# A four-layer graph network on one core: one more block by product in the last layer, and a rearranged preparation

## The chip, the core and the metric

The kernel runs on one core of a Trainium2 chip. The core has a matrix engine (TensorE, called PE in the profile, with its weight loads shown apart as PEld), three engines that work on elements (VectorE: DVE, ScalarE: ACT, GpSimd: POOL) and a queue that only issues transfers (SyncE: SP). The metric is the device time of one execution in microseconds; lower is better. The kernel before takes 2123.33 us (median of three runs, 2122.25 to 2134.76).

## The reference

There are 6250 nodes with 256 channels and 100,000 edges, sorted by destination. The input is normalised and passed through a relu; then come four graph layers, and the result is added to the input:

```python
def agg(h):
    return jax.ops.segment_sum(h[src], dst, num_segments=N)
for l in range(NL - 1):
    h = x + agg(x)
    h = jax.nn.relu(h @ W1s[l] + b1s[l])
    h = jax.nn.relu(h @ W2s[l] + b2s[l])
    x = h @ W3s[l] + b3s[l]
h = x + agg(x)
h = jax.nn.relu(h @ cW1 + cb1)
h = jax.nn.relu(h @ cW2 + cb2)
return h @ cW3 + cb3
```

All of it is float32. `NL` is 4, so three equal layers and a last one with a middle of 64 channels.

## The kernel before

**Blocks.** The nodes lie in 49 blocks of 128. The first product with W1 is pulled ahead of the sum over edges, so what a layer adds up over the edges is already a node's row times W1 (`w31` is the product of one layer's W3 and the next one's W1, made in the preparation by `fused`). A layer's rows stay on the chip in `XY`, each as a high part and a remainder, and also go to a table in memory, `tables[l]`.

**Two ways to sum over the edges.** For most blocks of destinations the kernel builds a matrix of edge counts (a destination block against all 49 source blocks, one byte an element) and multiplies it with `XY`. The matrices are built once, beside layer 0, by one-hot products (`build`: one-hots `lo` and `hi` at L1053 on DVE, products `bp` at L1094 on PE, casts to bytes at L1102 on ACT and L1104 on DVE), are used there where layer 0 needs them, and are stored in `mats` for the later layers (L1109). A layer reads them back in chunks (`fetch`, L1127), casts them (`prepare`, L1598) and multiplies: by panels of four blocks (`product`, L1700, 196 products of 128x512 for a panel), or for a single block (`product_by_node`, L1622, 49 products). In layer 0 all products are by node.

For the other blocks the rows of the sources are gathered from the table: 17 indirect transfers of 128 rows for each block, issued by POOL (`send`, L1407), and added up by PE with small one-hot products (`add`, L1446: 46 instructions, called a visit). `gone` lists the blocks whose edges are prepared for that, `solos[l]` those of them that layer l multiplies as single blocks instead. Gathered are 23 blocks in layer 0, 20 in layers 1 and 2, and 19 in layer 3 (blocks 0 to 17 and 48), where 18 and 19 are single products.

**Order of the work.** The order of instructions on each engine is written out when the program is made. One unit of time is one cast of a matrix piece and the products that use it; `tick` runs what is due in it: visits, turns (L1506), the layers' further products (`mlp`: L1248 or L1256, then L1268 or L1313) and stores. A clock in the model, `clock`, counts the costs of what PE has been given (`passed`). By it the gathers of a layer are asked for evenly: `begin` takes the model's work of the layer (`work_of`), less `TAIL[l]` and a margin of 6, less what has passed since the layer's first product, and divides it by the number of gathers. Each gather waits for the PE instruction at its place (`after`). A visit is due 6 us of model time after its last gather is asked for, at the latest `LATE[l]` units from the end of the layer's units. When all rows of a layer are in its table, the next layer's gathers begin.

For layer 3 the model's work before the change is 444.3 us: 30 blocks x 49 products of 512 columns, 19 visits and turns of 3.4, 45 + 5 blocks of further layers (19.35 + 8.6) and 7.8 for starts. With TAIL 10 it has 323 gathers to place. For layers 1 and 2, with 29 blocks, 20 visits and TAIL -5, it is 496.0 and 492.6, with 340 gathers.

**The preparation.** `look` finds the edges of each block by comparisons and asks for them; its last step turns the positions and indices (PE at L848) into `rel` and `idx` (DVE at L855 and L858), which the gathers need. Beside it `normed` goes through the blocks in pairs, one pair a step: moments (L892, L893), square root (L898), scale (L904, L905, L912), transposes (L921), product with W1 (L933), copy to `zs` (L945), high part (L949, ACT), remainder (L953, DVE), store to the table (`keep`, by SP). After the last pair's product, ten products whose result is not used stand in PE's queue (L939). The buffers of the preparation are given back when its last store has landed; the first one-hot of the gathers (L1430) and the building use that memory. The first 24 casts of the building all run on ACT.

`spare` is the memory of the positions `clT`, reused later for a few single results and the last layer's weights. Tiles named `align` only shift addresses.

## Time and profile before

| | us |
|---|---|
| median of three runs | 2123.33 |
| lowest and highest of them | 2122.25, 2134.76 |
| the profiled execution | 2128.08 |
| its span, first to last instruction | 2126.3 |
| PE busy, mean granted clock | 2034.3, 0.99 |

The profile shows one execution. Its times are microseconds from the first instruction. A group of instructions has a line of the code, an engine, an operation, its output and input, the shape and the count, then the busy time, the mean length of one in nanoseconds, and the idle time of the engine just before it, with what ended most of that. A row in order of time has start, length, engine, line and operation; what stands in brackets is the idle time before it and what ended it. The table by stretches gives, for each engine, its busy time in the stretch and its number of instructions, then the clock that was granted to PE (1.00 is full), the share of time in which the transfer engines were busy, and what they moved.

### The profile page before, as it was taken

How to read it: one execution, taken by the hardware profiler on the slowest of the kernel's cores; microseconds unless marked ns; L12 is line 12 of the kernel's file. 1: busy time of each engine (PE TensorE's matmuls, PEld its weight loads, DVE VectorE, ACT ScalarE, POOL GpSimd, SP SyncE). 2: the span in 40 equal slices, each digit the busy share in tenths (PEclk: the TensorE clock that was granted, in tenths of full speed). 3: DMA queues.
4: the chain of work that ended last, by engine and by line, in shares of the span. 5: the costliest groups of instructions: out<-in, count | busy, mean ns of one | idle time of the engine just before them, and what ended most of it. 6: DMA issues, size and time to landing. Idle time of an engine off the chain costs nothing.

```text
span 2126.3 us, 33236 instructions
## 1 busy us (share of the span) xinstructions
PE 2034.3 (96%) x12076; PEld 1495.9 (70%) x12076; DVE 925.0 (44%) x2103; ACT 872.8 (41%) x1793; POOL 1445.9 (68%) x1467
## 2 busy tenths in 40 slices
PE   6889999999999999999999999999999999989998
PEld 4657676667676777777777777777776767766665
DVE  6987767677662422232234322322233323223333
ACT  5766656456555433323233423232233322222222
POOL 3747777677774477777777477777776477777772
PEclk9989999999999999999999999999999999999999
DMA  5534455545455654555566554555555555555563
GB/s 174 159 117 148 145 156 150 157 139 162 140 161 168 205 163 145 160 177 161 154 184 202 171 165 149 176 166 158 169 171 176 173 170 185 161 184 185 154 189 109
DMA packets 184900, 347.54 MB, mean 163 GB/s; under 512 B 32446, under 2 KB 118496, under 8 KB 184726
## 3 DMA queue, kind: packets, MB, share of 16 engines
q0 software_dynamic: 68960, 185.36, 29.9%
q1 hardware_dynamic: 113838, 158.12, 22.8%
q8 instruction: 96, 1.57, 0.3%
q10 hardware_dynamic: 1928, 1.85, 0.3%
q14 instruction: 78, 0.64, 0.1%
HBM read 287.93 MB, written 57.26 MB: 162 GB/s over the span
## 4 chain that ended last, share of the span: by engine, by line
PE 86%; DMA 4%; DVE 3%; issue 1%; ACT 1%; POOL 1%; DVEq 0%; SPq 0%; POOLq 0%; ACTq 0%
PE agg L1700 43%; PE agg L1622 15%; PE sums L1446 11%; PE ps L1256 6%; PE ps L1313 6%; PE bp L1094 4%; DMA rows<-table,idx 4%; PE ps L1506 1%; DVE hi L1053 1%; POOL rows L1407 1%; DVE at L1104 1%; PE ps L1268 1%; PE ps L1248 0%; DVE lo L1053 0%; ACT at L1102 0%
## 5 line engine op out<-in xcount | busy, mean ns | idle before, releaser
L1407 POOL DMA_INDIRECT rows<-table,idx x1394 | 1388.8, 996 | 595.7 <-issue 225.7
L1700 PE MATMUL agg<-a,XY 128*128 128x512 f32 x4116 | 978.6, 395 | 1.9 <-DVE clT L1634 1.9
L1700 PEld LDWEIGHTS agg<-a,XY 128*128 128x128 f32 x4116 | 764.9, 188 | 192.7 <-issue 35.0
L1598 ACT CAST a<-at 128x512 fp32r<-128x512 uint8 (+1 forms) x542 | 328.7, 617 | 653.7 <-PE agg L1700 613.1
L1598 DVE CAST a<-at 128x512 fp32r<-128x512 uint8 x543 | 246.8, 456 | 515.7 <-PE agg L1700 479.1
L1622 PE MATMUL agg<-XY,a 128*128 128x512 f32 x1470 | 405.4, 410 | 1.7 <-ACT a L1582 1.0
L1622 PEld LDWEIGHTS agg<-XY,a 128*128 128x128 f32 x1470 | 260.0, 190 | 51.4 <-issue 6.6
L1446 PE MATMUL sums<-rows,hot 128*32 128x256 f32 x3772 | 248.3, 391 | 33.5 <-DMA rows<-table,idx 33.3
L1446 PEld LDWEIGHTS sums<-rows,hot 128*32 128x32 f32 x3772 | 124.0, 111 | 151.0 <-DMA rows<-table,idx 46.1
L1582 ACT CAST a<-at 128x512 fp32r<-128x512 uint8 (+2 forms) x362 | 197.2, 576 | 6.6 <-PE agg L1622 6.6
L1102 ACT CAST at<-bp 128x392 uint8<-128x392 f32 x252 | 121.5, 490 | 186.9 <-PE bp L1094 181.3
L1104 DVE CAST at<-bp 128x392 uint8<-128x392 f32 x228 | 128.6, 564 | 137.4 <-PE bp L1094 135.0
L1475 DVE TENSOR_TENSOR u<-u,sums 128x256 f32<-128x256 f32 x82 | 34.4, 419 | 301.3 <-PE agg L1700 273.6
L1094 PE MATMUL bp<-hi,lo 128*128 128x196 bf16 x960 | 128.3, 256 | 14.9 <-DVE hi L1053 13.3
L1313 PE MATMUL ps<-w,h 128*128 128x256 f32 x588 | 133.8, 379 | 1.4 <-ACT h L1259 0.9
L1053 DVE TENSOR_TENSOR hi<-cols,pairs 128x784 bf16<-128x784 bf16 x240 | 134.9, 562 | 0.0
L1256 PE MATMUL ps<-h,w 128*128 128x512 f32 (+3 forms) x332 | 133.8, 545 | 0.3 <-ACT h L1713 0.3
L1094 PEld LDWEIGHTS <-lo 128*128 128x128 bf16 x960 | 72.3, 100 | 83.5 <-DVE hi L1053 34.9
L1313 PEld LDWEIGHTS ps<-w,h 128*128 128x128 f32 x588 | 111.3, 190 | 18.5 <-ACT h L1259 1.4
L1321 DVE TENSOR_TENSOR zz<-ps,w 128x512 f32<-128x512 f32 (+1 forms) x75 | 50.2, 679 | 116.5 <-PE ps L1313 116.5
L1053 DVE TENSOR_TENSOR lo<-lanes,pairs 128x512 bf16<-128x512 bf16 x240 | 100.6, 419 | 0.7 <-issue 0.3
L1510 ACT ACTIVATE h<-ps,bias 128x256 f32<-128x256 f32 (+1 forms) x116 | 47.6, 464 | 128.5 <-PE ps L1506 128.5
(170 smaller groups left out, 962.6 us busy)
## 6 DMA issues: line engine op xcount, KB each, us to landing
at<-mat SPq DMA_DIRECT2D x151, 448.0 KB
mat<-at SPq DMA_DIRECT2D x30, 784.0 KB
rows<-table,idx POOLq DMA_INDIRECT x1394
table<-zz SPq DMA_DIRECT2D x72, 256.0 KB
back<-table SPq DMA_DIRECT2D x99, 128.0 KB
xs<-in_x_dram SPq DMA_DIRECT2D x8, 768.0 KB
table<-zs SPq DMA_DIRECT2D x24, 256.0 KB
out_dram<-zz SPq DMA_DIRECT2D x24, 256.0 KB
```

Of the source, the lines that this page charges most:

```text
L1053: nc.vector.tensor_tensor(o.rearrange("p q (n t) -> p q n t", t=2), values.rearrange("p (n t) -> p n t", t=2)[:, None, :, :].to_broadcast( ...
L1094: mm = nc.tensor.matmul(bp[:, m * HW:(m + 1) * HW], lo[:, q + m, :], hi[:, q + m, :], start=True, stop=True)
L1102: nc.scalar.copy(o, v)
L1104: nc.vector.tensor_copy(o, v)
L1256: mm = nc.tensor.matmul(ps[:mp, :w], weights[l][0][:, c, i * P:i * P + mp], h1[:, c, :w], start=(c == 0), stop=(c == KC - 1))
L1313: mm = nc.tensor.matmul(o, h2[0][:, c, nodes], w3[:, c, :], start=(c == 0), stop=(c == KC - 1))
L1407: got = nc.gpsimd.indirect_dma_start(out=t, out_offset=None, in_=tables[self.l][:, :], in_offset=bass.IndirectOffsetOnAxis(ap=idx[:, o:o + ...
L1446: nc.tensor.matmul(self.sums[m * Q:(m + 1) * Q, :C], self.hot[:, c - min(rounds), m, :], self.rows[g, c + 4 * m], start=(c == ROUNDS[0][0] ...
L1582: nc.scalar.copy(a[:, i * m * P:(i + 1) * m * P].rearrange("p (j d) -> p j d", j=m), counts[b][:, j:j + m, :])
L1598: cast(o, at[:, :, d:d + m * P])
L1622: mm = nc.tensor.matmul(agg, a[:, d:d + P], XY[:, j, :], start=(j == 0), stop=(j == NT - 1))
L1700: mm = nc.tensor.matmul(agg[c][:, :w], XY[:, j, o:o + P], a[:, :w], start=(at == 0 and half == 0), stop=(at == NT - 1 and half == 1))
```

## The change

**In the last layer** block 17 becomes a single product as well: `solos[3]` is 17, 18, 19, and 18 blocks are gathered, with 306 transfers. Its product stands behind that of the first panel. In the model the layer's work is then 452.4 us (31 blocks of products, 18 visits). `TAIL` of layer 3 goes from 10 to -3 and its `LATE` from -8 to -5; `TAIL` of layer 0 goes from 10 to 16.

**Beside layer 0** block 17's matrix is built too, as the 26th of 31, and the four blocks that are built only for later layers come at other places in the order.

**In the preparation** the moments of six blocks are put together in four operations of their own where each block had an aggregation; the high part, the remainder and the store are done for four blocks at a time; of the weights for the fused products one has a single buffer and is loaded after its last use; and the ten unused products behind the last pair become sixteen behind the turning of positions and indices.

```diff
-    solos = [[], [19], [19], [18, 19]]
+    solos = [[], [19], [19], [17, 18, 19]]
...
     for i in range(panels[-1][1]):
-        made.insert(6 * i + 5, panels[-1][0] + i)
+        made.insert((4, 9, 14, 19)[i], panels[-1][0] + i)
+    made.insert(25, 17)
...
     def fused(pool, w3_aps, w1_aps):
-        loaded = []
-        def load(l):
-            if l < NLAYER:
-                loaded.append((load_w("w3", w3_aps[l], pool, nc.scalar, bufs=2),
-                               load_w("w1n", w1_aps[l], pool, nc.scalar, bufs=2)))
-        load(0)
+        def left_of(l):
+            return load_w("w3", w3_aps[l], pool, nc.scalar, bufs=1) if l < NLAYER else None
+        def right_of(l):
+            return load_w("w1n", w1_aps[l], pool, nc.scalar, bufs=2) if l < NLAYER else None
+        w3, w1 = left_of(0), right_of(0)
         yield
         for l in range(NLAYER):
-            w3, w1 = loaded[l]
-            load(l + 1)
+            w1_next = right_of(l + 1)
...
                 nc.scalar.copy(w3t[:, k, :], ps[:, :C])
+            w3 = left_of(l + 1)
             yield
...
                 nc.vector.tensor_copy(o, ps[:, :left[NQ]])
+        still = ps_m.tile([P, W], F32, name="ps")
+        for _ in range(16):
+            nc.tensor.matmul(still, XY[:, 1, :P], XY[:, 0, :], start=True, stop=True)
         yield
...
         def moments(s):
             i0, n = pairs[s]
+            t0 = i0 // G * G
+            if i0 == t0:
+                each[t0] = pool.tile([P, G, 6], F32, name="stats", bufs=2)
             for i in range(i0, i0 + n):
-                stats = pool.tile([P, nc.vector.BN_STATS_DIM], F32, name="stats", bufs=4)
-                nc.vector.bn_stats(stats, xs[i // G * G][:, i % G, :])
-                nc.vector.bn_aggr(mv[:, i, :], stats)
+                nc.vector.bn_stats(each[t0][:, i - t0, :], xs[t0][:, i - t0, :])
             if (i0 + n) % G == 0 or i0 + n == NT:
...
+                nc.vector.tensor_tensor(apart[:, :m], v[:, :m, 1], v[:, :m, 4], OP.subtract)
+                nc.vector.tensor_tensor(both[:, :m, :], v[:, :m, 1:3], v[:, :m, 4:6], OP.add)
+                nc.vector.scalar_tensor_tensor(apart[:, :m], apart[:, :m], float(C // 4),
+                                               apart[:, :m], op0=OP.mult, op1=OP.mult)
+                nc.vector.tensor_tensor(both[:, :m, 1], both[:, :m, 1], apart[:, :m], OP.add)
                 std = pool.tile([P, G], F32, name="std", bufs=2)
-                nc.scalar.activation(std[:, :m], mv[:, t0:t0 + m, 1], AF.Sqrt, bias=eps)
+                nc.scalar.activation(std[:, :m], both[:, :m, 1], AF.Sqrt, bias=eps, scale=1.0 / C)
...
             paced[:] = [mm.ins.name]
-            if s == len(pairs) - 1:
-                still = ps_m.tile([P, W], F32, name="ps")
-                for _ in range(10):
-                    nc.tensor.matmul(still, XY[:, 1, :P], XY[:, 0, :], start=True, stop=True)
...
         def out(s):
-            zs[s] = pool.tile([P, 2, C], F32, name="zs", bufs=4)
+            i0, n = pairs[s]
+            if s % 2 == 0:
+                zs[s] = pool.tile([P, 4, C], F32, name="zs", bufs=3)
+            o = zs[s - s % 2][:, s % 2 * 2:s % 2 * 2 + n, :]
...
+        def four(s):
+            if s % 2 == 0 and s + 1 < len(pairs):
+                return None
+            i0 = pairs[s - s % 2][0]
+            return i0, pairs[s][0] + pairs[s][1] - i0, s - s % 2
+
         def high(s):
-            i0, n = pairs[s]
-            nc.scalar.copy(XY[:, i0:i0 + n, :C], zs[s][:, :n, :])
+            if four(s):
+                i0, n, k = four(s)
+                nc.scalar.copy(XY[:, i0:i0 + n, :C], zs[k][:, :n, :])
...
-        order = [[]] + [[0, 1, 2, 19, 3, 4, 5, 6]] * 2 + [[0, 1, 18, 2, 3, 19, 4, 5, 6]]
+        order = [[]] + [[0, 1, 2, 19, 3, 4, 5, 6]] * 2 + [[0, 17, 1, 18, 2, 3, 19, 4, 5, 6]]
...
-        TAIL = [10.0] + [-5.0] * (NLAYER - 1) + [10.0]
-        LATE = [-8] + [10] * (NLAYER - 1) + [-8]
+        TAIL = [16.0] + [-5.0] * (NLAYER - 1) + [-3.0]
+        LATE = [-8] + [10] * (NLAYER - 1) + [-5]
...
                 u = alone[l, b0] = late.tile([P, C], F32, name="us", bufs=1) if (
-                    k == 1) else spare[:, k // 2 * C:(k // 2 + 1) * C]
+                    k == 1) else spare[:, 3 * (k // 2) * C:(3 * (k // 2) + 1) * C]
...
-            rings.tile([P, 64], U8, name="align", bufs=1)
+            rings.tile([P, 192], U8, name="align", bufs=1)
...
-        rings.tile([P, 128], U8, name="align", bufs=1)
```

31 lines of the change are left out of this document (18 added, 13 removed).

## The prediction, made before the change was run

> **What bounds the kernel now.** The head of the page and its chain of waits come first.
>
> ```profile
> span 2126.3 us, 33236 instructions
> ...
> PE 2034.3 (96%) x12076; PEld 1495.9 (70%) x12076; DVE 925.0 (44%) x2103; ACT 872.8 (41%) x1793; POOL 1445.9 (68%) x1467
> ...
> PE 86%; DMA 4%; DVE 3%; issue 1%; ACT 1%; POOL 1%; DVEq 0%; SPq 0%; POOLq 0%; ACTq 0%
> ```
>
> TensorE (PE) is busy for 96% of the span and carries 86% of the chain, so an added product costs its length, and a gain has to come from stages where PE waits. The table by stretches shows where: the gathering parts of layers 1, 2 and 3 (columns: start:end, length, busy time of PE, its weight loads, DVE, ACT and POOL, granted clock, DMA share, GB/s).
>
> ```profile
> 735.00:1175.00 440.00, 439.59 (x2541) 328.38 (x2540) 132.64 (x278) 140.03 (x252) 321.79 (x327) 1.00 0.55 168
> 1215.00:1642.00 427.00, 422.05 (x2457) 313.19 (x2456) 124.71 (x263) 133.31 (x240) 321.64 (x325) 1.00 0.55 168
> 1690.00:2098.00 408.00, 381.66 (x2323) 279.24 (x2322) 124.02 (x253) 113.59 (x202) 303.41 (x306) 0.98 0.56 173
> ```
>
> In layer 1 PE idles 0.4 us of 440, in the last layer 26.3 of 408. The groups of PE in these three stretches name the waiter, the gathered sums (count, busy time, mean ns, idle before); the fourth row, also of the last stretch, is the product of the two single blocks.
>
> ```profile
> L1446 PE MATMUL sums<-rows,hot 128*32 128x256 f32 x920 | 56.6, 381 | 0.1
> ...
> L1446 PE MATMUL sums<-rows,hot 128*32 128x256 f32 x920 | 58.6, 382 | 4.9 <-DMA rows<-table,idx 4.9
> ...
> L1446 PE MATMUL sums<-rows,hot 128*32 128x256 f32 x874 | 66.6, 414 | 26.0 <-DMA rows<-table,idx 26.0
> L1622 PE MATMUL agg<-XY,a 128*128 128x512 f32 x98 | 23.5, 393 | 0.0
> ```
>
> An undisturbed visit of a block takes 56.6 / 20 = 2.83 us. The last layer's 19 visits should take 53.8; they take 66.6 and wait another 26.0. So 66.6 - 53.8 + 26.0 = 38.8 us are lost there, against 56.6 + 0.1 - 56.6 = 0.1 in layer 1 and 58.6 + 4.9 - 56.6 = 6.9 in layer 2.
>
> What the rows wait for is the issuing of the gathers on POOL (two groups, layers 1 and 3, then one gather of the last layer in order of time).
>
> ```profile
> L1407 POOL DMA_INDIRECT rows<-table,idx x327 | 322.3, 986 | 112.3 <-issue 52.7 <-PE agg L1700 48.3 <-PE ps L1256 4.6
> ...
> L1407 POOL DMA_INDIRECT rows<-table,idx x306 | 303.4, 992 | 99.5 <-issue 49.4 <-PE agg L1700 36.7 <-DMA rows<-table,idx 5.8
> ...
> 1669.66 0.95 POOL L1407 DMA_INDIRECT rows<-table,idx  x1 [0.30 <-issue]
> ```
>
> Even when it waits for nothing POOL needs 0.30 us between gathers, so one costs at least 0.992 + 0.30 = 1.292 us. In the last layer it takes (303.4 + 99.5) / 306 = 1.317: POOL is 98% committed. The asking rate follows from the constants. With the model's work of 444.3 us for the last layer and TAIL 10, 323 gathers are spread over 444.3 - 10 - 6 - x, where x is what the model's clock has passed between the layer's first product and its first gather (30 to 45, an estimate). That is 1.19 to 1.24 us a gather, faster than POOL can issue. In layer 1 the same formula gives (496 + 5 - 6 - x) / 340 = 1.32 to 1.37, slower than POOL needs, and there nothing waits. So the last layer is bound by POOL, the others by PE.
>
> **The change, part by part. Last layer.** Block 17 leaves the gathered ones: 17 gathers and one visit go (-2.8 us of PE), and one single product comes. Two took 23.5 us, so it costs +11.75. Its two chunk loads and 14 casts lie on SP, ACT and DVE, which are busy for under a third of that stretch. Its transposes are as many as before. The work in the model becomes 452.4, and with TAIL -3 the 306 gathers are spread over 452.4 + 3 - 6 - x: 1.32 to 1.37 us each, layer 1's rate to the second digit, above POOL's 1.292. The 38.8 us then shrink to what the other layers lose at that rate, 0.1 to 6.9; I take 4, nearer to layer 2, since POOL has only 3% to spare. Sum: 11.75 - 2.8 - 38.8 + 4 = -25.9 us; its ends are -30 (nothing lost) and about -11 (half of the loss stays).
>
> **Layer 0.** Block 17's matrix has to be built too (whole run, by groups, then 100 us of layer 0 by stretch).
>
> ```profile
> L1094 PE MATMUL bp<-hi,lo 128*128 128x196 bf16 x960 | 128.3, 256 | 14.9 <-DVE hi L1053 13.3
> ...
> L1053 DVE TENSOR_TENSOR hi<-cols,pairs 128x784 bf16<-128x784 bf16 x240 | 134.9, 562 | 0.0
> L1053 DVE TENSOR_TENSOR lo<-lanes,pairs 128x512 bf16<-128x512 bf16 x240 | 100.6, 419 | 0.7 <-issue 0.3
> ...
> 300.00:400.00 100.00, 97.62 (x655) 69.50 (x657) 67.36 (x152) 56.50 (x129) 73.28 (x74) 1.00 0.50 149
> ```
>
> One thirtieth of 128.3 + 14.9 is 4.8 us of PE. Part of that was run at a low clock (below), so I take +4, with ends 3 and 5. DVE gets 8 x (0.562 + 0.419) = 7.8 us of one-hots and some casts, beside a PE that is 98% busy while DVE is 67%: nothing on the path. If DVE were the limit, it would be these 8 us. The store of the matrix is one more SP transfer, read only in the last layer: nothing. Moving the spare blocks' building to other places between the products changes no amount; it costs nothing as long as POOL and DVE keep their slack.
>
> At the end of layer 0 its last visit waits for rows (PE, in order of time):
>
> ```profile
> 668.05 0.63 PE L1446 MATMUL sums<-rows,hot 128*32 128x256 f32 x6
> 671.07 4.46 PE L1446 MATMUL sums<-rows,hot 128*32 128x256 f32 x40 [2.38 <-DMA rows<-table,idx]
> ```
>
> From 668.05 to 675.53 it takes 7.48 us against 2.83. TAIL 16 for 10 ends the asking 6 us of model time sooner, which covers the 4.65 us; the rate over 391 gathers rises by under 2%. I take -4, with ends -4.7 and 0.
>
> **Preparation.** Two stretches, then groups of the preparation, the last but one a short form of the row before it:
>
> ```profile
> 20.00:60.00 40.00, 31.32 (x137) 24.04 (x137) 29.34 (x81) 32.85 (x68) 17.00 (x18) 1.00 0.48 141
> 60.00:110.00 50.00, 42.70 (x235) 33.23 (x233) 47.79 (x142) 38.70 (x87) 33.93 (x30) 1.00 0.49 149
> ...
> L893 DVE BATCH_NORM_AGGREGATE mv<-stats 128x2 f32<-128x6 f32 x49 | 8.9, 182 | 1.7
> L949 ACT CAST XY<-zs 128x512 fp32r<-128x512 f32 x24 | 14.8, 619 | 3.7 <-DVE zs L945 3.7
> L953 DVE TENSOR_TENSOR XY<-zs,XY 128x512 fp32r<-128x512 f32 x24 | 16.1, 670 | 4.5 <-ACT XY L949 4.4
> L953 DVE TENSOR_TENSOR XY<-zs,XY 128x256 fp32r<-128x256 f32 x1 | 0.4, 421 | 0.0
> L905 DVE SCALAR_TENSOR_TENSOR shift<-mv,rstd 128x6 f32<-128x6 f32 x8 | 1.4, 171 | 0.3
> ```
>
> DVE is busy for 47.8 of 50 us from 60 to 110 and sets the pace there. 49 aggregations (8.9 us) become 9 x 4 operations on six values, at the 0.171 of L905: 6.2, so -2.7. The 24 subtractions of L953 become 12 of double length: 0.670 + 2 x (0.670 - 0.421) = 1.17 us each, 14.0 for 16.1, so -2.1. ACT's casts shrink alike. The DVE stretch holds about half of the tiles: half of 4.8, that is -2.4 (ends 0 and -4.8). The third weight of each fused product now arrives in the one buffer left to it, asked for after its predecessor's transposes instead of a step earlier; ACT waits for those transposes anyway for its copy, but PE may stand for the load: +0.5 (ends 0 and +4). The stores, half as many and twice as large, go out on SP with no one behind them but the last, which is not enlarged.
>
> The end of the preparation, in order of time, then by stretch:
>
> ```profile
> 112.75 2.65 PE L939 MATMUL ps<-XY 128*128 128x512 f32 x10
> ...
> 115.24 0.70 PE L848 MATMUL ps<-ident,wd 68*128 68x68 f32 x7
> ...
> 115.97 1.08 DVE L855 TENSOR_SCALAR rel<-ps 128x100 bf16<-128x100 f32 x6 [1.72 <-PE ps L848]
> ...
> 120.03 0.96 DVE L1430 TENSOR_TENSOR hot<-colf,rel 128x768 f32<-128x768 f32 x1 [1.21 <-DMA table<-zs]
> ...
> 121.85 1.46 PE L1094 MATMUL bp<-hi,lo 128*128 128x196 bf16 x7 [5.24 <-DVE hi L1053]
> ...
> 124.00:134.00 10.00, 8.05 (x42) 4.10 (x39) 8.92 (x22) 8.79 (x24) 6.05 (x6) 0.50 0.54 172
> 134.00:139.50 5.50, 4.87 (x17) 3.36 (x17) 1.99 (x6) 3.29 (x8) 0.00 (x0) 0.50 0.01 4
> 139.50:145.00 5.50, 5.50 (x33) 4.16 (x32) 4.29 (x11) 4.25 (x10) 0.95 (x1) 1.00 0.00 0
> ```
>
> The ten idle products stand ahead of the transposes that DVE waits for. Without them the indices come 1.72 us sooner, and with them the last store, the gathers and the first one-hot, which all hang on it: -1.7 (ends 0 and -2.3). Sixteen of them behind the transposes run for 16 x 0.265 = 4.2 us into the idle 5.24. Now the granted clock falls to 0.50 in that gap and returns at 139.5: 17 matmuls take the 5.5 us in which 33 run later, so 5.5 x 16 / 33 = 2.7 us are lost; from 124 to 134 ACT is 88% busy and PE not the limit. With some 1 to 2 us of idleness left I expect the clock to stay: -2.5 (ends 0 and -3.9).
> [...]
>
> Preparation: -2.4 + 0.5 - 1.7 - 2.5 = -6.1.
>
> **The tail.** The last visit moves closer to the end (LATE -5 for -8, and later asking). Its chain, PE in order of time:
>
> ```profile
> 2094.35 2.80 PE L1446 MATMUL sums<-rows,hot 128*32 128x256 f32 x46
> ...
> 2110.88 0.70 PE L1310 MATMUL ps<-clT,h 64*128 64x256 f32 x2
> ```
>
> Now 16.5 us pass from that visit to the last step of block 48, and products follow it. With five units of four products (0.93 us each by 23.5 us / 98 matmuls) after the visit, block 48 ends beside the last panel's own layers: +1.5 (ends 0 and +6).
>
> **Sum:** -25.9 + 4 - 4 - 6.1 + 1.5 = -30.5 us. The profiled execution took 2128.08 us, 4.75 over the median of 2123.33 (three runs, 2122.25 to 2134.76); its stages are not longer in one place that I can see, so the sum goes to the median: 2093 us, 1.4% less.
>
> **The rivals.**
> *Rows later than paced (slower).* A slower rate also means that a visit's last gather is sent only 6 us of model time before the visit. The longest landing in the chain of waits is this (start, length):
>
> ```profile
> 2069.33 6.76 DMA rows<-table,idx
> ```
>
> With 1.3 us of issuing that is 8.1, over 2 us too late. If each of 18 visits waited w, the sum would be -30.5 - 4 + 18 w; it breaks even at w = 1.9 and is 1% slower from w = 3.1. A wait of 2.1 with the slow products behind it (4.46 for 40 in layer 0, where 2.46 is usual: +2) is 4.1 us, +39 us, 2162. Against it: layer 1 has the same margin and rate and loses 0.1 us in 20 visits. Chance 0.04.
>
> *POOL still short (within 1%).* The rate left is 3% above POOL's need, and the stretch of layer 2, whose formula differs by 0.01 us, already loses 6.9. If half of the loss stayed, 15 us of the gain would go: 2108. For it speaks that the added block puts its extra reading into the same layer; against it, that 17 gathers of 128 KB go for one matrix of 784 KB. Chance 0.18.
>
> *The preparation gives nothing* (the clock falls all the same, and PE waits for the weights): -24 us, 2099. Chance 0.13.
>
> *All of it gains:* nothing lost in the last layer, DVE's whole 4.8 us on the path: -40, 2083. Chance 0.08. The forecast itself: 0.57.
>
> **How the numbers follow.** About 1%, 21 us, is what a measurement of this kernel can tell from no change. The forecast lies beyond it by 9 us, so of its 0.57 some 0.52 are faster by over 1%; with 0.08 and most of 0.13 that is 0.71, and a margin for terms that I bounded on the cautious side makes it 0.74. Within 1%: 0.21. Slower: 0.05. The range leaves out the slow rival and the far ends: 2077 (-46, every end at its best) to 2111 (-12, half of the loss left).
>
> **What would show it.** In the profile of the changed kernel: gathered sums of 18 visits in the last layer, with idle time below 8 us and POOL idle beyond 0.30 us a gather; three single products of 11.75 us there; the last visit of layer 0 under 4 us; clock 1.00 between 120 and 140; the first build products before 120; no longer stretch between the last panel and the end than 12 us. The prediction is wrong if the sums of the last layer still wait for 20 us or more, or if the PE work of layer 0 grows by more than 6.

## The result and the profile after

| | before | after |
|---|---|---|
| median, us | 2125.13 (4 runs, 2122.25 to 2134.76) | 2103.84 (4 runs, 2103.32 to 2104.78) |
| the profiled execution, us | 2128.08 | 2104.15 |
| its span, us | 2126.3 | 2102.4 |

The ratio of after to before is 0.9893 with an interval of 0.9871 to 0.9915: 1.1% less, 21 us. Forecast were 2093 us, and a range of 2077 to 2111. The span became 23.9 us shorter where the sum said 30.5.

Lines moved: the gathers stand at L1427 after the change (L1407 before), the gathered sums at L1466 (L1446), single products at L1642 (L1622), panels at L1720 (L1700), building products at L1114 (L1094), one-hots at L1073 (L1053), the gathers' one-hots at L1450 (L1430), the remainders `zz` at L1341 (L1321), the idle products at L862. First the head of the page of after, then its table by stretches (start:end, length, busy PE, weight loads, DVE, ACT, POOL, granted clock, DMA share, GB/s) for the gathering parts of layers 1, 2 and 3, and then its groups of PE and of POOL in the last of the stretches.

```profile
span 2102.4 us, 33308 instructions
...
PE 2031.7 (97%) x12117; PEld 1501.4 (71%) x12117; DVE 933.8 (44%) x2108; ACT 879.7 (42%) x1799; POOL 1441.1 (69%) x1450
```

```profile
735.00:1175.00 440.00, 439.35 (x2539) 328.00 (x2538) 131.88 (x278) 139.90 (x252) 321.78 (x326) 1.00 0.55 168
1215.00:1642.00 427.00, 422.05 (x2459) 313.39 (x2458) 123.84 (x264) 133.14 (x240) 321.53 (x325) 1.00 0.55 168
1690.00:2080.00 390.00, 386.54 (x2362) 289.75 (x2361) 130.78 (x264) 120.33 (x213) 290.35 (x289) 1.00 0.57 178
```

```profile
L1466 PE MATMUL sums<-rows,hot 128*32 128x256 f32 x828 | 53.2, 382 | 3.5 <-DMA rows<-table,idx 3.3
L1642 PE MATMUL agg<-XY,a 128*128 128x512 f32 x147 | 35.4, 394 | 0.0
...
L1427 POOL DMA_INDIRECT rows<-table,idx x289 | 290.9, 1007 | 95.0 <-issue 51.2 <-PE agg L1720 34.4 <-PE agg L1642 5.5
```

Layers 1 and 2 are as before; the last layer now looks like layer 2. Its 18 visits take 53.2 us and wait 3.5, so 53.2 + 3.5 - 18 x 2.83 = 5.8 us are lost to rows, where 38.8 were. PE idles 3.5 us of 390. POOL spends (290.9 + 95.0) / 289 = 1.335 us on a gather, above the 1.31 (1.007 + 0.30) that it needs at least.

The rest of the change is seen in order of time: on PE the last visit of layer 0 and the end of the preparation (start, length, engine, line, operation; in brackets the idle time before).

```profile
109.74 0.81 PE L849 MATMUL ps<-ident,wd 68*128 68x68 f32 x7
...
112.00 3.91 PE L862 MATMUL ps<-XY 128*128 128x512 f32 x16 [0.76 <-DVE rel L856]
116.58 0.50 PE L1114 MATMUL bp<-hi,lo 128*128 128x196 bf16 x4 [0.68 <-DVE hi L1073]
117.40 0.50 PE L1114 MATMUL bp<-hi,lo 128*128 128x196 bf16 x4 [0.31 <-DVE hi L1073]
...
128.34 2.08 PE L1642 MATMUL agg<-XY,a 128*128 128x512 f32 x4 [1.03 <-ACT a L1602]
...
670.07 2.80 PE L1466 MATMUL sums<-rows,hot 128*32 128x256 f32 x46
```

The last visit of layer 0 runs through in 2.80 us (7.48 before). The positions are turned at 109.74 (115.24 before), the first building product comes at 116.58 (121.85), the first product of layer 0 at 128.34 (134.63). The idle products fill the gap; but the granted clock of after, by stretches, still falls:

```profile
120.00:125.00 5.00, 2.70 (x24) 1.54 (x22) 4.46 (x13) 4.45 (x13) 3.98 (x4) 1.00 0.35 110
125.00:130.00 5.00, 3.67 (x17) 2.12 (x15) 3.02 (x8) 4.79 (x11) 1.82 (x2) 0.56 0.63 213
130.00:135.00 5.00, 5.00 (x25) 3.63 (x25) 3.46 (x10) 2.76 (x6) 0.00 (x0) 0.76 0.00 0
```

**Where the 23.9 us come from.** Both spans are divided at the same events, all on PE.

| stretch | before | after | difference | forecast |
|---|---|---|---|---|
| preparation, to the first product of layer 0 | 134.63 | 128.34 | -6.3 | -6.1 |
| layer 0, to the first product of layer 1 | 556.18 | 559.74 | +3.6 | 0 (+4 - 4) |
| layers 1 and 2, to the end of layer 2's last visit | 950.70 | 952.63 | +1.9 | 0 |
| last layer, to the end of the last product | 474.85 | 445.69 | -29.2 | -25.9 |
| tail | 9.94 | 16.0 | +6.1 | +1.5 |
| span | 2126.3 | 2102.4 | -23.9 | -30.5 |

The tail of after, PE in order of time:

```profile
2083.39 3.01 PE L1720 MATMUL agg<-a,XY 128*128 128x512 f32 x12
2086.34 1.14 PE L1288 MATMUL ps<-clT,h 64*128 64x256 f32 x8
2089.12 0.65 PE L1276 MATMUL ps<-h,w 128*64 128x128 f32 x4 [1.65 <-DVE zz L1317]
2090.29 0.70 PE L1330 MATMUL ps<-clT,h 64*128 64x256 f32 x2 [0.51 <-ACT h L1279]
2090.91 1.08 PE L1268 MATMUL ps<-h,w 128*64 128x256 f32 x8
2092.63 0.70 PE L1288 MATMUL ps<-clT,h 64*128 64x256 f32 x2 [0.63 <-ACT h L1272]
2094.17 1.21 PE L1288 MATMUL ps<-clT,h 64*128 64x256 f32 x6 [0.84 <-DVE zz L1317]
```

The last product ends at 2086.4. Behind it come a step of two other blocks' layers (L1288), block 48's remaining layers (L1276, L1330), each waiting for its predecessor, and only then the last panel's (L1268 from 2090.91, 4.5 us behind the last product; before it was 0.3). Block 48 did not end beside the panel's layers but ahead of them in PE's queue. In the kernel before, the same three steps stand ahead of the last product (at 2104.23, 2108.23 and 2110.88), so the table counts their 2.5 us in the last layer there and in the tail here.

### The profile page after: what moved, and what is told of

Read it like the earlier page. It is cut to its first block, busy times and chain, and to the rows that moved or that the text cites. A ratio compares the mean times of both kernels' runs of the same rounds, so it can differ in the third digit from the quotient of the medians.

```text
span 2102.4 us, 33308 instructions
## 1 busy us (share of the span) xinstructions
PE 2031.7 (97%) x12117; PEld 1501.4 (71%) x12117; DVE 933.8 (44%) x2108; ACT 879.7 (42%) x1799; POOL 1441.1 (69%) x1450
## 3 DMA queue, kind: packets, MB, share of 16 engines
q1 hardware_dynamic: 114078, 159.72, 23.1%
q10 hardware_dynamic: 1928, 1.85, 0.3%
## 5 line engine op out<-in xcount | busy, mean ns | idle before, releaser
L1427 POOL DMA_INDIRECT rows<-table,idx x1377 | 1381.2, 1003 | 587.5 <-issue 225.4
L1720 PE MATMUL agg<-a,XY 128*128 128x512 f32 x4116 | 976.6, 394 | 1.9 <-DVE clT L1654 1.9
L1720 PEld LDWEIGHTS agg<-a,XY 128*128 128x128 f32 x4116 | 765.2, 188 | 190.1 <-issue 32.4
L1618 DVE CAST a<-at 128x512 fp32r<-128x512 uint8 (+1 forms) x550 | 251.0, 458 | 522.4 <-PE agg L1720 476.0
L1642 PE MATMUL agg<-XY,a 128*128 128x512 f32 x1519 | 420.9, 410 | 1.7 <-ACT a L1602 1.0
L1642 PEld LDWEIGHTS agg<-XY,a 128*128 128x128 f32 x1519 | 268.3, 189 | 54.2 <-issue 9.2
L1466 PE MATMUL sums<-rows,hot 128*32 128x256 f32 x3726 | 233.4, 381 | 8.7 <-DMA rows<-table,idx 8.5
L1466 PEld LDWEIGHTS sums<-rows,hot 128*32 128x32 f32 x3726 | 118.5, 109 | 117.1 <-issue 27.6
L1114 PE MATMUL bp<-hi,lo 128*128 128x196 bf16 x992 | 129.5, 251 | 16.9 <-DVE hi L1073 16.1
L1073 DVE TENSOR_TENSOR hi<-cols,pairs 128x784 bf16<-128x784 bf16 x248 | 139.1, 561 | 0.0
L1276 PE MATMUL ps<-h,w 128*128 128x512 f32 (+3 forms) x332 | 133.7, 545 | 2.0 <-DVE zz L1317 1.7
L1114 PEld LDWEIGHTS <-lo 128*128 128x128 bf16 x992 | 72.8, 98 | 87.7 <-DVE hi L1073 37.3
L1073 DVE TENSOR_TENSOR lo<-lanes,pairs 128x512 bf16<-128x512 bf16 x248 | 103.6, 418 | 0.2 <-issue 0.2
L1341 DVE TENSOR_TENSOR zz<-ps,w 128x512 f32<-128x512 f32 (+1 forms) x75 | 50.2, 678 | 117.1 <-PE ps L1333 117.1
```

Of the source, the lines that this page charges most:

```text
L1073: nc.vector.tensor_tensor(o.rearrange("p q (n t) -> p q n t", t=2), values.rearrange("p (n t) -> p n t", t=2)[:, None, :, :].to_broadcast( ...
L1114: mm = nc.tensor.matmul(bp[:, m * HW:(m + 1) * HW], lo[:, q + m, :], hi[:, q + m, :], start=True, stop=True)
L1276: mm = nc.tensor.matmul(ps[:mp, :w], weights[l][0][:, c, i * P:i * P + mp], h1[:, c, :w], start=(c == 0), stop=(c == KC - 1))
L1427: got = nc.gpsimd.indirect_dma_start(out=t, out_offset=None, in_=tables[self.l][:, :], in_offset=bass.IndirectOffsetOnAxis(ap=idx[:, o:o + ...
L1466: nc.tensor.matmul(self.sums[m * Q:(m + 1) * Q, :C], self.hot[:, c - min(rounds), m, :], self.rows[g, c + 4 * m], start=(c == ROUNDS[0][0] ...
L1618: cast(o, at[:, :, d:d + m * P])
```

## The experiments

Four questions: do the parts of the change add up; what makes layer 0 longer; what do the new places of the spare blocks do; and can tail and clock be had as well. Each batch also ran the kernel before: 2126.81 us in the batch of the first four experiments (17 runs), 2127.88 and 2126.88 in the last two. The kernel after was not run again in them; times are set against its 2103.84 us, ratios against its 0.9893 (0.9871 to 0.9915).

**The preparation alone.** The kernel before with the new preparation; blocks, places, `TAIL` and `LATE` are the old ones. The diff shows this as an edit of the kernel after.

```diff
-    solos = [[], [19], [19], [17, 18, 19]]
+    solos = [[], [19], [19], [18, 19]]
...
-        TAIL = [16.0] + [-5.0] * (NLAYER - 1) + [-3.0]
-        LATE = [-8] + [10] * (NLAYER - 1) + [-5]
+        TAIL = [10.0] + [-5.0] * (NLAYER - 1) + [10.0]
+        LATE = [-8] + [10] * (NLAYER - 1) + [-8]
```

> The kernel before with the new preparation alone (moments by six, rows by four, one buffer for a weight, sixteen idle products last); building, order, TAIL and LATE as before. Theory A, the parts add up: the first product of layer 0 starts 6.3 us earlier, as it did with the whole change, and all that follows is only shifted; the last visit of layer 0 still waits some 4 us; 6 us less than before, 0.997. Theory B, layer 0 swallows what the preparation gives, because its end is set by gathers on POOL: the first product of layer 0 is 6 us earlier, the first of layer 1 by less than 2, and the time is that of before within 2 us.

Measured: 2120.61 us, ratio 0.9974 (0.9964 to 0.9985), 6.2 us below the 2126.81 beside it. The first product of layer 0 comes at 129.36, 5.3 earlier than before (expected were 6.3), and layer 0 takes 556.57 (556.18 before). The gain stays; no later stage takes it back, as theory A has it. That start differs from one profiled execution to the next: in the six profiles of this preparation on chips as fast as the first it lies between 127.77 and 129.36.

**The last layer alone.** The kernel before with block 17 as a product, the new places and the new last layer; the preparation and layer 0's `TAIL` stay.

```diff
-    solos = [[], [19], [19], [18, 19]]
+    solos = [[], [19], [19], [17, 18, 19]]
...
-        made.insert(6 * i + 5, panels[-1][0] + i)
+        made.insert((4, 9, 14, 19)[i], panels[-1][0] + i)
+    made.insert(25, 17)
...
-        TAIL = [10.0] + [-5.0] * (NLAYER - 1) + [10.0]
-        LATE = [-8] + [10] * (NLAYER - 1) + [-8]
+        TAIL = [10.0] + [-5.0] * (NLAYER - 1) + [-3.0]
+        LATE = [-8] + [10] * (NLAYER - 1) + [-5]
```

> The kernel before with block 17 as a product alone: solos, order of building, order of products, TAIL -3 and LATE -5 of the last layer; the preparation and TAIL 10 of layer 0 as before. Theory A, the parts add up: the last layer gives back 29 us up to its last product and its end takes 6 more, layer 0 takes 8 more up to the first product of layer 1: 15 us less than before, 0.993. Theory B, layer 0's extra time comes from its earlier start (a better preparation runs into the same limit there): layer 0 takes 4 us more, 19 us less than before, 0.991.

Measured: 2111.71 us, ratio 0.9926 (0.9908 to 0.9945): -15. With the preparation's -6 that makes -21, as much as the whole change gains. So the parts add up within the few us that the intervals leave, and layer 0's `TAIL` of 16, which is in neither run, adds little. Layer 0 takes 561.51 us, 5.3 more than before and between the two theories, with the old wait of its last visit still in it (7.45). The groups of the building products in layer 0, before, in this kernel and in after, say what the added matrix costs (busy, mean ns, idle before):

```profile
L1094 PE MATMUL bp<-hi,lo 128*128 128x196 bf16 x912 | 118.4, 251 | 7.9 <-DVE hi L1053 7.2 <-ACT at L1102 0.3
```

```profile
L1095 PE MATMUL bp<-hi,lo 128*128 128x196 bf16 x944 | 122.9, 250 | 10.0 <-DVE hi L1054 8.9 <-ACT at L1103 0.3 <-DVE at L1105 0.2
```

```profile
L1114 PE MATMUL bp<-hi,lo 128*128 128x196 bf16 x944 | 122.7, 250 | 12.4 <-DVE hi L1073 11.7 <-DVE at L1124 0.2 <-ACT at L1122 0.2
```

The products themselves grow by 4.3 to 4.5 us, the forecast's 4. Their waits for one-hots grow too: by 2.1 us here and by 4.5 in after, where `TAIL` is 16. So the asking that ends sooner removes 4.65 us at the last visit, and layer 0 becomes only 561.51 - 559.74 = 1.8 us shorter by it (the starts of the two differ in clock as well, 0.71 in 135 to 140 here, 0.56 in 125 to 130 and 0.76 in 130 to 135 in after, so part of the rest may lie there).

**The old places with the added matrix.** The kernel after, with the spare blocks at their old places in the order of building.

```diff
-        made.insert((4, 9, 14, 19)[i], panels[-1][0] + i)
+        made.insert(6 * i + 5, panels[-1][0] + i)
```

> The changed kernel with the four spare blocks built at their old places (after 5, 11, 17, 23) and block 17 at place 25 as in the change. Theory A, the new places crowd VectorE: the waits of the build products on the one-hots hi fall from 11.7 us back to 8, layer 0 is 4 us shorter, 2100 us. Theory B, the thirty-first block costs this wherever it is built: layer 0 as long as in the changed kernel within 1 us, 2104 us.

Measured: 2132.43 us, ratio 1.0025 (1.0015 to 1.0036), 28.6 us over the kernel after. Neither theory had that. Layer 0 takes 588.67 us, 28.9 more than in after; 21.4 of them are idle time ahead of the building products (33.8 for 12.4), and PE's busy time there grows by 8.0 (552.3 for 544.3), which was not traced further. The group of the building products in layer 0, then 6 us of it in order of time, PE and DVE:

```profile
L1114 PE MATMUL bp<-hi,lo 128*128 128x196 bf16 x944 | 125.5, 253 | 33.8 <-DVE hi L1073 32.2 <-ACT at L1122 0.6 <-DVE at L1124 0.2
```

```profile
334.27 0.51 PE L1114 MATMUL bp<-hi,lo 128*128 128x196 bf16 x4
335.56 0.34 PE L1114 MATMUL bp<-hi,lo 128*128 128x196 bf16 x2 [0.77 <-DVE hi L1073]
```

```profile
334.61 0.42 DVE L1073 TENSOR_TENSOR lo<-lanes,pairs 128x512 bf16<-128x512 bf16 x1
334.94 0.56 DVE L1073 TENSOR_TENSOR hi<-cols,pairs 128x784 bf16<-128x784 bf16 x1
335.41 0.56 DVE L1124 CAST at<-bp 128x392 uint8<-128x392 f32 x1
335.89 0.42 DVE L1073 TENSOR_TENSOR lo<-lanes,pairs 128x512 bf16<-128x512 bf16 x1
```

A building step is two products; DVE makes the two one-hots for two steps at a time and casts every second result. Here it works without a gap, 1.28 us for two steps (from 334.61 to 335.89: two one-hots and a cast), and PE waits for the one-hots. By the table of stretches DVE is busy for 65.3 us of 300 to 400: the average says that there is room, and the stretch of a few units says that there is none.

Why there is none can be read from the program. Each unit of layer 0 has a goal of building steps; it takes at most three at once, and stops where the next matrix has no free buffer of the three. A matrix that is built ahead of its use holds a buffer, the following steps are put off, and are then made up three in a unit. Counted in the written order, of the 337 units of layer 0 those with three steps are 8 in the kernel before, 7 after, and 63 with the old places and the 31st matrix. The spare blocks' new places are not decoration: with block 17 built at its place, the change gains only because they moved.

**The old asking in the last layer.** The kernel after with `TAIL` 10 and `LATE` -8 in the last layer: block 17 is a product, but the gathers are asked for sooner and done earlier.

```diff
-        TAIL = [16.0] + [-5.0] * (NLAYER - 1) + [-3.0]
-        LATE = [-8] + [10] * (NLAYER - 1) + [-5]
+        TAIL = [16.0] + [-5.0] * (NLAYER - 1) + [10.0]
+        LATE = [-8] + [10] * (NLAYER - 1) + [-8]
```

> The changed kernel with TAIL 10 and LATE -8 in the last layer, as before, so that the gathers of 18 blocks are asked for every 1.29 to 1.33 us, at POOL's own 1.29. Theory A, what counts is the number of gathers and the rate is second: waits in the last layer's visits of 8 to 15 us instead of 6, the end after the last product 4 to 6 us shorter than 16, the time within 4 us of the changed kernel. Theory B, the slower rate made the gain: waits of over 25 us come back, 2120 us or more.

Measured: 2106.04 us, ratio 0.9899 (0.9875 to 0.9923), which can't be told from the change. Theory A had that, nearly to the figure. Underneath two things cancel: the last layer is 7.4 us longer (453.1 for 445.7) and the tail 6.4 shorter (9.6 for 16.0). The last layer's sums and gathers:

```profile
L1466 PE MATMUL sums<-rows,hot 128*32 128x256 f32 x828 | 54.2, 383 | 4.7 <-DMA rows<-table,idx 4.7
...
L1427 POOL DMA_INDIRECT rows<-table,idx x290 | 290.3, 1001 | 91.0 <-issue 47.2 <-PE agg L1720 33.7 <-PE agg L1642 4.3
```

The visits lose 54.2 + 4.7 - 18 x 2.83 = 8.0 us, 2.2 more than in after; 2.5 of the 7.4 are the three steps that stand ahead of the last product again. Last layer and tail together took 484.8 us before, 462.7 here and 461.7 in after. So nearly all of the gain, 22 of 23 us, comes from the block that isn't gathered. POOL's pace is nearly the same in all three: a gather takes (290.3 + 91.0) / 290 = 1.315 us of it here, 1.317 before and 1.335 in after, each within 2% of what it needs at least. What the layer gets back is about the time of the 17 gathers that it no longer holds, 17 x 1.317 = 22 us.

**Four edits on a slower chip.** Even places (3, 8, 13, 19 and block 17 at 24, with no unit of three steps), no idle products, `TAIL` 4 and `LATE` -8 in the last layer, and `TAIL` 10 in layer 0, each alone, went to a chip on which the kernel before took 2369.74 us.

```diff
-        made.insert((4, 9, 14, 19)[i], panels[-1][0] + i)
-    made.insert(25, 17)
+        made.insert((3, 8, 13, 19)[i], panels[-1][0] + i)
+    made.insert(24, 17)
```

> The changed kernel with the spare blocks built at places 3, 8, 13, 19 and block 17 at 24: by the program's own plan no unit of layer 0 then has to take three building steps to catch up, against 7 in the changed kernel, 8 before and 63 with the old places and block 17. Theory A, the catching up is what makes PE wait for the one-hots: the waits of the build products in layer 0 fall from 11.7 us to 8 or less, and the time by 2 to 4 us, 2100 us. Theory B, the waits come from VectorE's load as such: they stay above 10, the time within 1 us.

```diff
-        still = ps_m.tile([P, W], F32, name="ps")
-        for _ in range(16):
-            nc.tensor.matmul(still, XY[:, 1, :P], XY[:, 0, :], start=True, stop=True)
```

> The changed kernel without the sixteen idle products. Theory A, they keep the clock over the gap before the building: without them PE idles for some 5 us from 111, the clock falls there and stays low until 133 or later, and the first product of layer 0 starts 0.5 to 1.5 us later, the time grows by 1 to 3 us. Theory B, the clock falls during the building anyway, so they are worth nothing: low for as long as with them (8 us), the time within 0.5 us.

```diff
-        TAIL = [16.0] + [-5.0] * (NLAYER - 1) + [-3.0]
-        LATE = [-8] + [10] * (NLAYER - 1) + [-5]
+        TAIL = [16.0] + [-5.0] * (NLAYER - 1) + [4.0]
+        LATE = [-8] + [10] * (NLAYER - 1) + [-8]
```

> The changed kernel with TAIL 4 and LATE -8 in the last layer, between before and after. Theory A, the end and the waits are traded against each other: end after the last product 10 to 12 us (16 in the changed kernel, 9.6 with TAIL 10), waits in the last layer's visits 6 to 9 us, 2 to 4 us less than the changed kernel, 2101 us. Theory B, every us taken from the end comes back as waiting: 2104 us within 1.

```diff
-        TAIL = [16.0] + [-5.0] * (NLAYER - 1) + [-3.0]
+        TAIL = [10.0] + [-5.0] * (NLAYER - 1) + [-3.0]
```

> The changed kernel with TAIL 10 in layer 0, as before. Theory A, the earlier asking removes the wait of layer 0's last visit and costs some of it in waits of the build products before it: layer 0 takes 561.5 us instead of 559.7, the last visit 7.5 instead of 2.8, the time 2 us more. Theory B, the full wait comes back: 4.5 us more.

Measured: 2342.07 (0.9893, 0.987 to 0.9915), 2342.01 (0.988, 0.9847 to 0.9913), 2340.18 (0.9889, 0.9863 to 0.9916) and 2341.31 (0.9879, 0.985 to 0.9908). All four intervals overlap, and hold the change's own ratio: nothing is told apart by time. The list of PE's waits of the third of them shows one part of why the scale is another (us in all, times, longest):

```profile
PE sums L1466 <- issue: 54.4, 95, 2.4
```

Such waits (95 of them here), in which PE waits for nothing that the profile shows, don't appear in that list for the kernel after on the other chip. Two things can still be read. With `TAIL` 4 the tail is 10.0 us, with -3 in the other three 16.0 to 16.8; and with `TAIL` 10 in layer 0 the last visit there waits for rows again (3.40 us). The first three were taken up again.

**All repairs together.** The kernel after with the even places, `TAIL` 4 and `LATE` -8 in the last layer, and in the first building one unused product of 512 columns behind each pair of building steps.

```diff
-        made.insert((4, 9, 14, 19)[i], panels[-1][0] + i)
-    made.insert(25, 17)
+        made.insert((3, 8, 13, 19)[i], panels[-1][0] + i)
+    made.insert(24, 17)
...
-        TAIL = [16.0] + [-5.0] * (NLAYER - 1) + [-3.0]
-        LATE = [-8] + [10] * (NLAYER - 1) + [-5]
+        TAIL = [16.0] + [-5.0] * (NLAYER - 1) + [4.0]
+        LATE = [-8] + [10] * (NLAYER - 1) + [-8]
...
+            still = ps_m.tile([P, W], F32, name="ps")
             while now[0] < PRE:
                 for _ in range(2):
                     next(beside)
                     built[0] += 1
+                nc.tensor.matmul(still, XY[:, 1, :P], XY[:, 0, :], start=True, stop=True)
```

> The changed kernel with three edits together: spare blocks built at 3, 8, 13, 19 and block 17 at 24 (no catching up in the plan), TAIL 4 and LATE -8 in the last layer, and one idle product after each two building steps at the start of the building. Theory A, each wins a little: the clock stays 1.00 from 115 to 140, 2 to 3 us; waits for one-hots in layer 0 8 us or less instead of 11.7, 2 to 4 us; the end after the last product 10 to 12 us instead of 16 with 6 to 9 us of waits in the visits, 2 to 4 us: 6 to 10 us less than the changed kernel, 2094 to 2098 us, or 0.985 of before. Theory B, one engine's slack is another's wait and the sum stays: 2102 us or more, 0.989.

Measured: 2090.78 us (2089.48 to 2094.87), ratio 0.9833 (0.982 to 0.9846), 13 us below the change, the fastest kernel here and faster than either theory had. Its span is 14.7 shorter than that of after: 4.5 in layer 0 (1.9 of them in its first 12 us, where the clock stays), 2.6 in layers 1 and 2, 1.5 in the last layer, 5.9 in the tail, 0.2 in the preparation. Of the 2.6, 1.6 are the clock at the opening of layer 1 (1.00 from 680 to 705 where after has 0.78 in 690 to 695; last section), at which none of the three edits aims. Its granted clock by stretches, and the first product of layer 0:

```profile
120.00:125.00 5.00, 4.00 (x29) 2.42 (x26) 4.46 (x12) 4.34 (x14) 4.09 (x4) 1.00 0.40 122
125.00:130.00 5.00, 3.93 (x26) 2.52 (x25) 3.15 (x8) 5.00 (x12) 1.75 (x2) 1.00 0.62 200
```

```profile
128.12 1.20 PE L1642 MATMUL agg<-XY,a 128*128 128x512 f32 x4 [0.93 <-ACT a L1602]
```

With the unused products PE is busy for 4.0 us of the five from 120, where it was 2.7 in after, and the clock stays at 1.00. The first four products take 1.20 us for 2.08.

**Even places alone.** The edit of the first of the four above, on a chip like the first.

> [...] Theory A: waits of the build products for one-hots in layer 0 8 us or less, the first product of layer 1 2 to 4 us earlier than 688.1, 2100 us. Theory B: waits above 10, 2104 us within 1.

Measured: 2100.11 us, ratio 0.987 (0.9855 to 0.9885); the interval meets that of the change. PE waits 9.7 us for one-hots in layer 0 instead of 11.7, and the layer takes 558.10 for 559.74, between the two theories. The seven units of three steps were worth about 2 us, and 17 waits of about 0.6 us stay without any such unit. Most of those have another neighbour: 13 of the 17, 8.6 of the 9.7 us, end within 2.5 us of the start of one of two long operations of DVE that aren't the building's, a one-hot of the gathers (L1450, 0.95 us) or a remainder (L1341, 1.28 us for two). Of all building products only a fifth have one so near. One such place, DVE and then PE:

```profile
492.02 1.28 DVE L1341 TENSOR_TENSOR zz<-ps,w 128x512 f32<-128x512 f32 x2
...
493.55 0.56 DVE L1073 TENSOR_TENSOR hi<-cols,pairs 128x784 bf16<-128x784 bf16 x1
...
494.16 0.51 PE L1114 MATMUL bp<-hi,lo 128*128 128x196 bf16 x4 [1.09 <-DVE hi L1073]
```

That these operations cause the waits is read from the order of DVE's work; no run moved them.

**`TAIL` 4 and `LATE` -8 alone**, likewise.

> [...] Theory A, the end and not the pace is what is left to gain in the last layer: end after the last product near 10 us instead of 16, the stretch from the last visit of layer 2 to the last product no longer than the changed kernel's 445.7, 5 to 7 us less than the changed kernel, 2097 to 2099 us. Theory B, what the end gives comes back as waits: 2103 us or more.

Measured: 2097.74 us (2096.64 to 2100.19), ratio 0.9865 (0.9848 to 0.9881), 6.1 below the change, as theory A has it; the interval still touches that of the change, and the profile shows where the time went. The gathered sums of its last layer, and its tail in order of time:

```profile
L1466 PE MATMUL sums<-rows,hot 128*32 128x256 f32 x828 | 52.7, 382 | 2.3 <-DMA rows<-table,idx 2.3
```

```profile
2080.38 0.65 PE L1276 MATMUL ps<-h,w 128*64 128x128 f32 x4
...
2083.02 0.70 PE L1330 MATMUL ps<-clT,h 64*128 64x256 f32 x2
2083.65 1.20 PE L1720 MATMUL agg<-a,XY 128*128 128x512 f32 x4
2085.16 1.26 PE L1268 MATMUL ps<-h,w 128*64 128x256 f32 x8 [0.31 <-ACT h L1733]
```

Block 48's layers (L1276, L1330) lie between the last products again, and the tail is 9.85 us for 16.0. The last layer is hardly longer for it, 446.3 us for 445.7, though it holds the 2.5 us of those steps again, and the visits still lose only 52.7 + 2.3 - 18 x 2.83 = 4.1 us. The change's `TAIL` of -3 and `LATE` of -5 overshoot: with 4 and -8 no more is lost to rows, and the last visit isn't late. Which of the two constants does it was not tried apart.

**No idle products**, likewise, on that chip.

> [...] Theory A: the clock falls near 114 and stays low until some 132, first product of layer 0 0.5 to 1.5 us later, 1 to 3 us more than the changed kernel, 2105 to 2107 us. Theory B: no later and no slower within 0.5 us, 2104 us.

Measured: 2106.06 us, ratio 0.9905 (0.9888 to 0.9922), 2.2 over the change with intervals that overlap. PE at the end of its preparation in order of time, then by stretches:

```profile
116.47 1.62 PE L1111 MATMUL bp<-hi,lo 128*128 128x196 bf16 x8 [5.34 <-DVE hi L1070]
118.28 1.65 PE L1111 MATMUL bp<-hi,lo 128*128 128x196 bf16 x8 [0.19 <-ACT at L1119]
120.16 1.65 PE L1111 MATMUL bp<-hi,lo 128*128 128x196 bf16 x8 [0.24 <-ACT at L1119]
...
129.24 2.08 PE L1639 MATMUL agg<-XY,a 128*128 128x512 f32 x4 [1.03 <-ACT a L1599]
```

```profile
112.00:114.00 2.00, 0.00 (x0) 0.00 (x0) 2.00 (x4) 0.41 (x1) 0.00 (x0) 0.55 0.82 271
114.00:120.00 6.00, 3.27 (x16) 1.92 (x16) 5.14 (x12) 3.25 (x9) 3.42 (x4) 0.50 0.45 153
```

The clock falls some 1 us into the gap of 5.34 us (0.55 on average in 112 to 114), and by the second row the building goes on at half. Yet PE at half clock nearly keeps up: eight products (four building steps) take 1.88 us (118.28 to 120.16), where at full clock, in after, they take 1.63 (117.40 to 119.03) and PE waits for one-hots in between. The three kernels compared now turn the positions within 0.12 us of each other (109.62 to 109.74), so their starts can be set side by side. The first four products of layer 0 end at 131.32 here, at 130.42 in after (128.34 + 2.08) and at 129.32 with all repairs (128.12 + 1.20). So a clock that stays is worth 2.0 us up to there, and the sixteen idle products get 0.9 of them. In the time of the whole kernel that can't be told from nothing.

## Why the prediction was right in its sign and 11 us too low

Of the 11 us, 4.75 are the base. The sum was made against the profiled execution of 2128.08 and then taken from the median of 2123.33. Three runs were too few for that choice: the kernel before took 2126.81, 2127.88 and 2126.88 in the later batches. From 2128.08 the same sum gives 2097.6. The remaining 6.6 are terms of the sum. (The range was a little wider than its terms: their own ends add up to -43 and -15 us, where -46 and -12 were taken, and "all of it gains" to -37, not -40. The result lies inside either way.)

- **Last layer, -25.9: right in mechanism, -29.2 measured.** The waits left were 5.8 us for a forecast of 4, and three single products took 35.4 us, 11.8 each, as forecast. Of the 3.3 us beyond the sum 2.5 are the three steps that moved out of the stretch into the tail. The slower asking was not needed for it: with the old `TAIL` the forecast's formula asks for the 306 gathers every 1.28 to 1.33 us, and 22 of the 23 us came as well. Last layer and tail together gave -23.1 for a forecast of -24.4.
- **The tail, +1.5: mis-sized, +6.1 measured**, just past its upper end of +6. The step "block 48 ends beside the last panel's own layers" failed: in PE's written order block 48's steps stand ahead of the panel's, and their waits for DVE and ACT (1.65 and 0.51 us) lie bare. The panel's first step had nothing left to wait for (with `TAIL` 4 and `LATE` -8 it starts 0.3 us behind the last product), and yet it starts 4.5 us behind. (The products' unit there is 0.96 us by the figures given, not 0.93, which changes nothing.) `TAIL` 4 and `LATE` -8 alone gave all of it back.
- **Layer 0, +4 for building: half of it was missing.** Products grew by 4.3 us, but the waits for one-hots by 4.5. The step that failed is "beside a PE that is 98% busy while DVE is 67%: nothing on the path". An average over 100 us hid the two or three microseconds at a time in which DVE is the limit. Units of three steps are one such place: even places, without any, took 2.1 us away. They are not the growth itself, since the kernel before has 8 of them and after 7. Most of the other waits stand behind a long operation of DVE for the gathers or the layers; that added one-hots make these collisions more frequent fits the rows, but was not shown.
- **"Moving the spare blocks' building to other places ... changes no amount; it costs nothing":** it costs nothing, but this was the part on which the rest stood. Left where they were, the change would have been no gain (1.0025). Nothing in the forecast gave the places a price; the written schedule, with its three buffers and its three steps a unit, would have.
- **The last visit of layer 0, -4: right where it was looked at** (2.80 us for 7.48), and little of it arrives: the last layer alone and the whole change differ by 1.8 us in layer 0, since the waits for one-hots are longer with `TAIL` 16. Why the two are linked was not tried; the gathers' one-hots on DVE, which move with the asking, are one candidate.
- **Preparation, -6.1: -6.3 measured (-5.3 with the preparation alone), by errors that cancel.** Up to the first building product the forecast was -2.4 + 0.5 - 1.7 = -3.6; measured are 116.58 - 121.85 = -5.3. The transposes of the positions begin at 109.74 where before the ten idle products began at 112.75: 3.0 us from the shorter work for a forecast of 2.4 (1.9 to 3.6 in the six profiles, so the two can't be told apart), and no wait of PE or ACT for a fused weight is in the lists, so the +0.5 was none. The other 2.3 are the idle products ahead of the transposes, forecast as 1.7 with 2.3 as the end.
- **The clock, -2.5: -1.0** (the rest of the -6.3). It was expected to stay at 1.00 with 1 to 2 us of idleness left. That was the author's estimate, and no run shows the 2.5 us: no gap in the first building of after exceeded 1.13 us, and the clock fell all the same, at about 125.6 (0.90 in 124 to 126, 0.50 in 126 to 128), where before it had fallen at about 119 (0.75 in 118 to 120). Had it stayed, about 2 us would have come, by the 2.0 between the run without idle products and the one with all repairs. The forecast looked at the gap alone; the building behind it, with PE busy for little more than half of the time (2.19 and 2.44 us of each 4 from 116 to 124), is the step that it left out.
- **Layers 1 and 2, 0: +1.9**, of which 1.6 come in the first 20 us of layer 1, where the clock falls in after (0.78 in 690 to 695) and not in before (1.00; last section).

Of the rivals, rows later than paced did not occur (3.5 us of waits in the last layer), POOL did not stay short (5.8 us lost for 38.8), and the preparation gave its gain though the clock fell. Of the signs named, these came: idle time of the sums below 8 us, POOL idle beyond 0.30 us a gather (0.33, but it was 0.33 before too, so this sign tells nothing), products of 11.8, last visit of layer 0 under 4, first building products before 120. Not: clock 1.00 between 120 and 140, and no stretch over 12 us behind the last product (16.0). The condition that PE's work in layer 0 grows by more than 6 is met only if its waits are counted: 4.3 + 4.5.

## What to carry to other kernels

An engine's average load says little about a hand-written schedule that works in bursts: before calling an added step free, count in how many units the feeding engine gets more than it can do in one, what buffers force that, and which long operations stand in its queue beside it. Work that ends last should be priced in the order in which the queue holds it, with its waits bare, not beside what it could overlap with. A sum made from one profiled execution belongs to that execution's time, unless many runs say that it was an outlier.

## What the runs showed of the hardware

**The clock fell with no wait above 1.13 us.** From 116 to 124 in after, PE was busy for 2.19 and 2.44 us of each 4, in pieces of 0.50 with waits of 0.30 between most of them, and the granted clock fell at about 125.6 (0.90 in 124 to 126, 0.50 in 126 to 128). It also fell between 125 and 129 in the profiles of the preparation alone (0.83 in 125 to 130, 0.50 in 130 to 135), the even places (the same two figures) and `TAIL` 4 (0.50 in 125 to 130). With the old places and the old asking the lengths of the products show it: with the old places four building products took 0.51 us at 124.74 and eight 1.65 without a wait from 125.55 (1.65 at a clock of 0.50 without idle products), with the old asking four took 0.52 at 127.19, and the first four products of layer 0 then took 2.07 and 2.08 (1.20 with all repairs, where the clock stayed). With unused products between the pieces (4.00 us busy of the 5 from 120) it stayed at 1.00, in the one profile there is of that. The busy share alone doesn't tell these cases apart: there too PE was busy for only 2.44 of the 4 us from 124, at a clock of 1.00. The forecast had one long wait in view, and after has none there; what makes the clock fall is not shown. Nor was the time to the fall the same each time. Taken from the average of the stretch in which it fell, as one step from 1.00 to 0.50, an estimate, the clock fell 2.4 us into the gap before the first building in the kernel before (gap from 116.61, 0.75 in 118 to 120), 4.1 us into the same gap with the last layer alone (from 116.68, 0.58 in 120 to 125), and 1.1 us into that without idle products (from 111.13, 0.55 in 112 to 114).

**The same wait, with and without a fall.** At the opening of layer 1 PE waits 1.85 us in both kernels; before kept its clock (1.00 in every stretch of 5 us from 680 to 705), after lost it (0.88 in 685 to 690, then 0.78). Before, PE in order of time, then after, and the stretch of after in which the clock was lowest:

```profile
690.81 1.21 PE L1700 MATMUL agg<-a,XY 128*128 128x512 f32 x4 [1.85 <-DVE clT L1634]
691.86 3.62 PE L1313 MATMUL ps<-w,h 128*128 128x256 f32 x16
```

```profile
688.08 1.51 PE L1720 MATMUL agg<-a,XY 128*128 128x512 f32 x4 [1.85 <-DVE clT L1654]
689.39 5.01 PE L1333 MATMUL ps<-w,h 128*128 128x256 f32 x16
```

```profile
690.00:695.00 5.00, 5.00 (x20) 4.17 (x19) 1.25 (x2) 0.00 (x0) 0.00 (x0) 0.78 0.14 50
```

Sixteen products took 5.01 us for 3.62. Behind the same wait of 1.85 us the fall also showed with the last layer alone (0.77 in 695 to 700), the old asking (0.66 in 690 to 695, the sixteen products 5.30 us), the even places (0.81 in 685 to 690, 5.18), `TAIL` 4 (0.82 in 685 to 690, 5.09) and no idle products (0.75 in 690 to 695, 4.72), but not with the preparation alone, the old places or all repairs together (1.00 in the stretches there, 3.62 in each). What decides between the two is not shown. On the sixteen products it is worth 1.1 to 1.7 us, and no edit of this study was made for it.

**One chip was 11% slower**: 2369.74 us against 2125 to 2128 for the kernel before. In the profiles of the four variants there PE is idle for tens of microseconds that the profile puts down to "issue" (45.6 to 54.6 us ahead of the gathered sums), and with `TAIL` 10 in layer 0 the products of these sums also took 307.6 us for 233.4 in after. What PE waits for is not shown; the cause stays open. The ratios of after's variants there, 0.9879 to 0.9893, are close to after's own on its chip, 0.9893.
